# Folded Fourier weights and re-placed expert steps in a six-block macaron kernel

## The chip, the cores and the metric

The kernel runs on one core of one Trainium2 chip, all in float32. The metric is the time of the whole program on the device in microseconds (us), as the median of several runs; lower is better.

## The reference, cut to what matters

Six residual blocks run on x of shape (8, 256, 128): feed-forward 1 (six nodes of 8-head attention), attention, feed-forward 1 again, experts, a mixer, and the same experts again. The change touches the last three and the end of the block before them.

```python
# experts (twice): LN(x) -> top 2 of 8
logits = xf @ gate_w;  scores = softmax(logits);  top_scores, top_idx = top_k(scores, 2)
h = silu(xs @ w1) * (xs @ w3)          # xs = xf scaled by the gate of each expert
x = x + 0.5 * (h @ w2).sum(experts)

# mixer: LN(x)
xz = einsum('bld,ed->bel', hidden, in_proj_w)             # 2 * 256 channels
out, out_b = selective scans of xz, forwards and backwards (16 states a channel)
x, z = split(xz)
xf = fftn(x, axes=(-2, -1))                               # over channels and tokens
xc = concatenate([xf.real, xf.imag], axis=1)              # 512 channels
xc = silu(conv1d(xc, fft_conv_w, 5 taps) + fft_conv_b)
x_out = ifftn(complex(*split(xc)));  v = abs(x_out * max(silu(z)))
y = out + out_b reversed + whitened v
x = x + y @ out_proj_w
```

The transform over channels, the input projection and the 5-tap convolution are all linear. So the kernel never transforms channels at run time: it composes, once, the matrix that leads from the 128 model features through the projection and the channel transform into the 512 outputs of each convolution tap (`w["conv"]`).

## The kernel before, in words

The 2048 tokens are four chunks of 512 (`NCH` = 4, `CT` = 512), each of four tiles of 128 (`NT` = 4). Feed-forward, attention and feed-forward run one after the other, each with a loop over `i` in which the order on TensorE (PE), VectorE (DVE) and ScalarE (ACT) is written out by hand. A dictionary `beside` puts steps of the next block's start into chosen `i`: `for_experts` prepares chunk 0 of the experts (LN statistics, scaling, transposes) at 46, 47 and 48 of the second feed-forward block, whose loop ends at 50.

`experts_and_mixer` runs the last three blocks as one list of slots. `at(slot, f, ...)` files a step under a slot, before or (with `last=True`) after the slot's scan sums. In each slot i the order is: scan of unit i (DVE, L1187) with its product with C (POOL, L1189); the product of unit i+1 with B (`feed`, DVE, L1176); the steps filed before; in odd slots the sums over states (`sums`, PE, L1206); the steps filed after; then `spread(i+2, i+4)`, PE products that broadcast rows for later units (L1158), and the exponentials of unit i+4 on ACT (L1166). The order on PE, DVE, ACT and POOL is exactly this; the SP queue, which issues the DMAs, is ordered by the framework's planner. There are 128 units, 32 a chunk (slots 0 to 127). Negative slots are the head; slots from 128 are the tail.

In the head stand:

- `taps` (L820, L827), which builds the short convolutions' weights, slots -28 to -25;
- the first experts, `first.step(n)` in slot n - 25, n = -2 to 17. A step n does the hidden products of tile n (`hidden`: PE L967, gate product `hid` on DVE L972, silu on ACT L975, product on POOL), closes tile n-2 (`close`: PE L993, x on DVE L997) and transposes tile n-1 (`turn`: PE L984, ACT copy L985). `early` and `late` put the preparation of the next chunk between the steps: statistics, scaling, transposes (L921), logits (L926) with their exponential (L937), and gates (L942 to L956);
- the mixer's start for chunk 0: `normalize`, `features`, four `convolve` (L1050), two `gate` products (L1037), `silu`, `ranks` (L1080), `steps` (L1101), `softplus` (L1114), `delta` (L1121, with two `du` DMAs), `rows` (sixteen small DMAs for B and C of each direction);
- the Fourier weights: `fetch` loads a tap's 1 MB into the tag `f8` (two buffers), `transform` (L839) applies the channel transform to the projection, and `conv_weights(tap, i)` (L868) multiplies the two, ten times, in slots -10 to -1: four 128-row pieces each, read by ACT (L876, L879) or by two DVE instructions (L882, L883).

All these small products use one PSUM tile, tag `p`, with one buffer (`bank`), so that each waits until the one before has been read.

In the tail the second experts' steps stand in slots n + 129, and their preparation, chunk by chunk, is in the same `early` and `late`: chunk 0 in slots 125 to 128, chunks 1 to 3 between the steps. ACT holds one table of functions at a time: Silu, Exp and Ln, and Sqrt need different ones, and a load appears in the trace as ACT_TABLE_LOAD (1.28 us). `exponentials()` loads the one for Exp and Ln ahead of time, at the end of `silu` and of `magnitude`.

Of the kernel before, what the change touches and what calls it, by code (L numbers as in the profile page):

```python
# [758 lines left out]


# [4 lines left out]
def experts_and_mixer(nc, tc, ident, nhalf, x, cols, ins, w, expert_xT, store):  # L765
# [19 lines left out]
    with ExitStack() as ctx:  # L785
# [4 lines left out]
        A = pool.tile([P, 2, 2, 4, 4], F32, name="A")  # L790
        Af = A.rearrange("p r t i j -> p (r t i j)")
        nc.scalar.activation(Af, A_log, AF.Exp)
        nc.vector.tensor_scalar(Af, Af, -1.0, -1e-25, ALU.mult, ALU.min)
# [39 lines left out]
        def transform():  # L833


            pf = bank([P, 4, D])
            for k in range(4):
                for t in range(2):
                    nc.tensor.matmul(  # L839
                        pf[:, k, :],  # L840
                        fold["FA"][:, t, k * P : (k + 1) * P],
                        fold["in_x"][:, t, :],
                        start=(t == 0),
                        stop=(t == 1),
                    )
            fold["fw"] = fw = pool.tile([P, 2, 6, D], F32, tag="t3", name="fw")
            for h, scale in enumerate((1.0, 0.5)):
                nc.scalar.mul(fw[:, h, 0:4, :], pf, scale)
                nc.scalar.mul(fw[:, h, 4:6, :], pf[:, 2:4, :], -scale)

        def fetch(tap):
            if tap is None:
                fold["FA"] = pool.tile([P, 2, 2 * S], F32, tag="mag", name="s_FA")
                nc.sync.dma_start(out=fold["FA"], in_=ins["s_FA"])
                fold["in_x"] = pool.tile([P, 2, D], F32, tag="mix0", name="s_in_x")
                nc.sync.dma_start(out=fold["in_x"], in_=ins["s_in_x"])
                return
            fold[tap] = pool.tile([P, 4, 2 * DI], F32, tag="f8", name="s_fft", bufs=2)
            nc.sync.dma_start(out=fold[tap], in_=ins["s_fft"][:, tap])

        def conv_weights(tap, i):
# [5 lines left out]
            for k, part in enumerate(((0, 1, 2, 3), (4, 5, 0, 1))[i]):  # L867
                nc.tensor.matmul(  # L868
                    pw,
                    fold["fw"][:, int(tap != 2), part, :],  # L870
                    fold[tap][:, k, :],
                    start=(k == 0),
                    stop=(k == 3),
                )
# [12 lines left out]
        class Experts:  # L887

            def __init__(self, xT=None, store=None):
                self.store = store
                self.chunks = [{} for _ in range(NCH)]
                if xT is not None:
                    self.chunks[0]["xT"] = xT
                self.tiles = [{} for _ in range(NCH * NT)]

            def early(self, n):
                c, i = n // NT + 1, n % NT
                if not 0 <= c < NCH:  # L900
                    return
                got = self.chunks[c]
                if i == 0:
                    got["stats"] = ln_scales(nc, pool, nhalf, x[c], 1e-5)
                elif i == 1:
                    both = pool.tile([P, 2, CT], F32, tag="dA", name="xn_xT", bufs=4)
                    got["xn"] = both[:, 0, :].rearrange("p (t d) -> p t d", t=NT)
                    got["xT"] = both[:, 1, :]
                    ln_scaled(nc, x[c], got["xn"], got["stats"])
                elif i == 3:  # L910
                    self.gates(got)

            def late(self, n):
                c, i = n // NT + 1, n % NT
                if not 0 <= c < NCH:
                    return
                got = self.chunks[c]
                if i == 1:
                    pt = bank([P, NT, P])
                    for t in range(NT):  # L920
                        nc.tensor.transpose(pt[:, t, :], got["xn"][:, t, :], ident)  # L921
                    nc.scalar.copy(got["xT"], pt.rearrange("p t l -> p (t l)"))
                elif i == 2:
                    pg = bank([P, NT, E])
                    for t in range(NT):
                        nc.tensor.matmul(  # L926
                            pg[:, t, :],
                            got["xT"][:, t * P : (t + 1) * P],
                            w["gate"],
                            start=True,  # L930
                            stop=True,
                        )
                    nmax = pool.tile([P, NT, 1], F32, tag="nmax", name="nmax")
                    nc.vector.tensor_reduce(nmax, pg, AX.X, ALU.max)
                    got["eg"] = eg = pool.tile([P, NT, E], F32, tag="eg", name="eg")
                    nc.vector.tensor_tensor(eg, pg, nmax.to_broadcast([P, NT, E]), ALU.subtract)
                    nc.scalar.activation(eg, eg, AF.Exp)  # L937

            def gates(self, got):
                eg = got["eg"]  # L940
                den = pool.tile([P, NT, 1], F32, tag="den", name="den")
                nc.vector.tensor_reduce(den, eg, AX.X, ALU.add)  # L942
                nc.vector.reciprocal(den, den)

                sc = pool.tile([P, NT, 2 * E], F32, tag="sc", name="sc")
                nc.gpsimd.memset(sc[:, :, E:], -1.0)
                nc.vector.tensor_tensor(sc[:, :, 0:E], eg, den.to_broadcast([P, NT, E]), ALU.mult)
                best = pool.tile([P, NT, 8], F32, tag="best", name="best")
                for t in range(NT):
                    nc.vector.max(best[:, t, :], sc[:, t, 0:E])  # L950
                nc.vector.memset(best[:, :, 2:8], -1.0)
                mark = pool.tile([P, NT, 2 * E], F32, tag="mark", name="mark")
                for t in range(NT):
                    nc.vector.match_replace(mark[:, t, :], best[:, t, :], sc[:, t, :], -2.0)
                got["gate"] = gate = pool.tile([P, NT, E, 1], F32, tag="gate", name="gate", bufs=2)
                nc.vector.scalar_tensor_tensor(  # L956
                    gate[:, :, :, 0], mark[:, :, 0:E], -2.0, sc[:, :, 0:E], ALU.is_equal, ALU.mult
                )
# [43 lines left out]
            def step(self, n):  # L1002
                self.early(n)
                self.hidden(n)
                if 0 <= n - 1 < NCH * NT or 0 <= n - 2 < NCH * NT:
                    pa = ps.tile([P, 2, CT], F32, tag="a", bufs=1, name="pa")
                    self.close(n - 2, pa)
                    self.turn(n - 1, pa)
                self.late(n)
# [3 lines left out]
        def normalize(ch, part):  # L1013
# [6 lines left out]
            if h == 0:  # L1020
                got["xn"] = expert_xT.rearrange("p (t d) -> p t d", t=NT)
# [42 lines left out]
        def silu(*tiles):  # L1064
# [6 lines left out]
            exponentials()  # L1071
# [336 lines left out]
        first, second = Experts(xT=expert_xT), Experts(store=store)  # L1408
        for n in range(-NT, NCH * NT + 2):
            if n >= -2:  # L1410
                at(n - 25, first.step, n)
            at(n + NCH * UNITS + 1, second.step, n)
# [7 lines left out]
        for k, (tap, i) in enumerate(order):  # L1420
            at(-10 + k, conv_weights, tap, i)
            if i == 1 and k < 6:
                at(-10 + k, fetch, order[k + 4][0])

        for ch in range(NCH):

            o = (ch - 1) * UNITS
            if ch == 0:
# [6 lines left out]
                at(-10, gate, ch, 1)  # L1435
                at(-9, silu, u_of(ch, 0), u_of(ch, 1), sz_of(ch))
# [4 lines left out]
                at(-7, steps, ch, 0, 1, last=True)  # L1441
                at(-6, softplus, ch)
            else:
# [9 lines left out]
                at(o + 20, silu, u_of(ch, 0), u_of(ch, 1), sz_of(ch), sc_of(ch - 1, 0))  # L1453
                at(o + 21, largest, ch)
# [33 lines left out]
            at(k, silu, *(sc_of(ch, co) for co in range(0 if final else 1, 4)))  # L1488
            at(k + 1, halves, ch, 0)
# [54 lines left out]
    "s_FA": (P, 2, 2 * S),  # L1544
# [8 lines left out]
def tile_kernel(ctx: ExitStack, tc: tile.TileContext, ins, out):  # L1553
# [28 lines left out]
    expert_xT = cpool.tile([P, CT], F32, name="first0")  # L1582

    with tc.tile_pool(name="w_ffn", bufs=1) as fp:
        hand = [expert_xT, *(fp.tile([P, CT], F32, name=f"first{i}") for i in (1, 2))]
# [29 lines left out]
        def for_experts(ps, bufs):  # L1615
# [4 lines left out]
            to_features(nc, ps, ident, tiles[1], expert_xT, bufs=bufs)  # L1620
# [22 lines left out]
        ffn(nc, tc, ident, nhalf, x, made.w, hand[0], steps(for_experts, 46, 47, 48))  # L1643
    with tc.tile_pool(name="w_mixer", bufs=1) as wp:
# [4 lines left out]
        experts_and_mixer(nc, tc, ident, nhalf, x, cols, ins, w | w_moe, expert_xT, store)  # L1649


def layout(i):
# [52 lines left out]
    fft = tiles(np.transpose(i["L1_attn_fft_conv_w"], (1, 2, 0)))  # L1705
    a["s_fft"] = np.swapaxes(fft, 1, 2)
    phase = 2 * np.pi * (np.outer(np.arange(S), np.arange(S)) % S) / S
    c, s = np.cos(phase), np.sin(phase)
    a["s_FA"] = tiles(np.concatenate([c, -s], 1).astype(np.float32))
# [57 lines left out]
```

## Time and profile before

| What | Value |
|---|---|
| Median of 3 runs | 2143.36 us (2140.32 to 2144.17) |
| The profiled execution | 2135.52 us, its span 2133.7 us |
| Mean granted TensorE clock | 0.964 |
| PE, DVE, ACT, POOL busy | 92%, 73%, 54%, 37% of the span |
| Head: 1394 to 1490 us | PE busy 77.4 of 96 us, DVE 19.2, ACT 30.5, POOL 10.4 |
| Last units: 1984 to 2046 us | PE busy 53.8 of 62 us, DVE 48.9, ACT 26.4, POOL 50.8 |
| Tail: 2070 to 2134 us | PE busy 45.4 of 64 us, DVE 23.4, ACT 25.2, POOL 20.6 |

The page gives busy times over the whole span; the view by windows gives them for a stretch, with the granted clock; the chain of waits follows the work that ended last back to its releasers; the timeline lists instructions in order of time with the idle time ahead of each and who ended it. All times of views are counted from the start of the span.

### The profile page before, as it was taken

Reading aid. Unit: us, or ns where it says so; the run is one execution under the profiler, and the core shown is the slowest. Engines: PE = TensorE matmul, PEld = TensorE weight load, DVE = VectorE, ACT = ScalarE, POOL = GpSimd, SP = SyncE. Lnnn points to the kernel's source line nnn. Section 1 sums busy time; section 2 is a strip of 40 time slices with the busy share of each in tenths; the row PEclk is TensorE's granted clock in tenths of the full one; section 3 lists DMA queues with packets and bytes.
Section 4 is the critical chain, followed back from the end, with each engine's and each line's share of the span. In section 5 each row is a group of like instructions: output and inputs, shape, how many; then the busy total and the mean of one; then the engine's idle time right before and its main releaser. Section 6 shows DMA issues by size and latency. Waiting matters only on the chain.

```text
span 2133.7 us, 45254 instructions
## 1 busy us (share of the span) xinstructions
PE 1962.1 (92%) x17868; PEld 1140.0 (53%) x17868; DVE 1548.6 (73%) x2651; ACT 1155.7 (54%) x2206; POOL 797.5 (37%) x916
## 2 busy tenths in 40 slices
PE   7999999998999999999999997787898988989976
PEld 5666666654566666666666654542233334334444
DVE  5777777777877776777777785412987978888853
ACT  3777777752323322677777763433455555654543
POOL 3000001036666655000000013311758968778852
PEclk9999999999999999899999997999998999999989
DMA  3000000000000000000000002002001000010000
GB/s 140 3 3 3 3 3 3 3 3 1 2 2 2 2 2 2 2 3 3 3 3 3 3 2 88 0 25 64 10 11 30 1 20 21 2 39 1 1 6 16
DMA packets 21076, 28.32 MB, mean 13 GB/s; under 512 B 12352, under 2 KB 13888, under 8 KB 20224
## 3 DMA queue, kind: packets, MB, share of 16 engines
q1 hardware_dynamic: 20576, 25.22, 4.0%
q8 instruction: 142, 2.33, 0.5%
q14 instruction: 70, 0.57, 0.1%
q10 hardware_dynamic: 288, 0.20, 0.0%
HBM read 15.17 MB, written 1.05 MB: 8 GB/s over the span
## 4 chain that ended last, share of the span: by engine, by line
PE 79%; DVE 8%; ACT 6%; POOL 3%; issue 3%; DMA 1%; DVEq 0%; ACTq 0%; SPq 0%; POOLq 0%
PE sc L339 20%; PE pc L378 9%; PE sc L607 6%; PE pp L294 6%; PE pU L1158 4%; PE pc L666 3%; PE p L1250 3%; PE pp L578 2%; PE p L1050 2%; PE ph L967 2%; PE py L1206 2%; PE pp L312 2%; PE p L868 2%; DVE h L1187 2%; PE pp L419 2%
## 5 line engine op out<-in xcount | busy, mean ns | idle before, releaser
L345 DVE TENSOR_REDUCE negmax<-sc 128x2 f32<-128x512 f32 x768 | 490.8, 681 | 161.2 <-PE sc L339 160.9
L350 ACT ACTIVATE ex<-sc 128x512 f32<-128x512 f32 x768 | 421.0, 609 | 197.3 <-PE sc L339 196.9
L339 PE MATMUL sc<-qk,qk 32*128 32x256 f32 x6144 | 474.1, 407 | 8.6 <-DVE negmax L345 7.5
L339 PEld LDWEIGHTS sc<-qk,qk 32*128 32x128 f32 x6144 | 298.0, 187 | 144.4 <-ACT ex L350 102.8
L1189 POOL TENSOR_TENSOR hc<-h,C 128x1024 f32<-128x1024 f32 x128 | 301.5, 2359 | 103.5 <-DVE h L1187 97.8
L1187 DVE TENSOR_TENSOR_SCAN h<-dA,pU 128x1024 f32<-128x1024 f32 x128 | 292.1, 2282 | 15.3 <-POOL hc L1189 2.3
L300 ACT ACTIVATE qk<-pp,w_bqk,head_rows 128x256 f32<-128x256 f32 x384 | 197.2, 572 | 78.0 <-PE pp L420 34.6
L86 POOL TENSOR_SCALAR ln_ve<-ln_mv 128x2 f32<-128x2 f32 (+1 forms) x56 | 12.6, 224 | 582.3 <-DVE ln_mv L84 580.5
L1166 ACT ACTIVATE dA<-pA,A 128x512 f32<-128x512 f32 x256 | 161.9, 684 | 87.4 <-PE pA L1158 87.3
L378 PE MATMUL pc<-ex,va 128*32 128x256 f32 x3072 | 205.2, 385 | 0.2 <-DVE y L443 0.2
L1176 DVE TENSOR_TENSOR pU<-pU,B 128x1024 f32<-128x1024 f32 x128 | 155.5, 1215 | 59.2 <-PE pA L1158 58.7
L1158 PE MATMUL pU<-du,s_sel 32*128 32x512 f32 x512 | 166.8, 664 | 18.8 <-DVE h L1187 18.2
L622 ACT ACTIVATE ex<-sc 128x512 f32<-128x512 f32 x128 | 66.1, 603 | 205.1 <-PE sc L607 205.1
L1158 PE MATMUL pA<-dl,s_sel 32*128 32x512 f32 x512 | 152.9, 671 | 6.5 <-ACT dA L1166 6.5
L607 PE MATMUL sc<-rot,rot 32*128 32x256 f32 x2048 | 135.2, 388 | 1.9 <-POOL rot L590 1.9
L378 PEld LDWEIGHTS pc<-ex,va 128*32 128x32 f32 x3072 | 80.5, 109 | 96.0 <-issue 61.1
L607 PEld LDWEIGHTS sc<-rot,rot 32*128 32x128 f32 x2048 | 97.9, 184 | 36.8 <-issue 23.1
L199 POOL TENSOR_SCALAR w_bqk<-pb,head_rows 128x2 f32<-128x2 f32 x12 | 3.5, 314 | 302.1 <-DVE pb L196 295.2
L625 POOL TENSOR_TENSOR both<-ex 128x512 f32<-128x512 f32 x64 | 80.0, 1271 | 71.5 <-ACT ex L622 71.5
L1158 PEld LDWEIGHTS pU<-du,s_sel 32*128 32x128 f32 x512 | 48.2, 193 | 97.4 <-issue 77.2
L972 DVE TENSOR_TENSOR hid<-ph,gate 128x1024 f32<-128x1024 f32 x32 | 39.1, 1223 | 80.8 <-PE ph L967 79.4
L617 DVE TENSOR_REDUCE anegmax<-sc 128x2 f32<-128x512 f32 x128 | 79.4, 683 | 25.1 <-PE sc L607 25.1
(274 smaller groups left out, 3209.9 us busy)
## 6 DMA issues: line engine op xcount, KB each, us to landing
qk<-turned SPq DMA_DIRECT2D x768, 1.0 KB
s_fft<-s_fft SPq DMA_DIRECT2D x5, 1024.0 KB
du<-ab SPq DMA_DIRECT2D x16, 256.0 KB
B<-low SPq DMA_DIRECT2D x64, 32.0 KB
C<-low SPq DMA_DIRECT2D x64, 32.0 KB
x<-x SPq DMA_DIRECT2D x4, 256.0 KB
out<-x SPq DMA_DIRECT2D x4, 256.0 KB
weT<-ffn_weT SPq DMA_DIRECT2D x1, 960.0 KB
```

What stands on the lines that cost most here:

```text
L294: nc.tensor.matmul(pp, w["qk"][:, c, i, :], src, start=True, stop=True)
L300: nc.scalar.activation(t[:, g, :], pp, AF.Identity, scale=w["mask"][:, g : g + 1], bias=w["bqk"][:, c, i, g : g + 1],)
L339: nc.tensor.matmul(sc[:, t, :], lhs[:, t * P : (t + 1) * P], rhs, start=True, stop=True)
L345: nc.vector.tensor_reduce(sh[:, :, 4 * g + j], sc, AX.X, ALU.max, negate=True)
L350: nc.scalar.activation(ex, sc, AF.Exp, scale=FD**-0.5)
L378: nc.tensor.matmul(st["pc"][32 * j : 32 * j + 32, g, :], st[2][:, kt, 2 * j + g, :], st["ex", g, j][:, kt, :], start=(kt == 0), stop=(kt = ...
L607: nc.tensor.matmul(sc[j][:, t, :], lhs[r, part, t * P : (t + 1) * P] if part < 2 else sel[r, :], rhs[r, part, :] if part < 2 else st["nm"] ...
L1158: nc.tensor.matmul(dst[:, jj, :], w["sel"][rs, i, :], src[rs, :], start=True, stop=True)
L1166: nc.scalar.activation(dA[:, jj, :], pA[:, jj, :], AF.Exp, scale=A[:, r, t, i, j : j + 1])
L1176: nc.vector.tensor_tensor(dB, dB, bcast(gots[ch]["B", r], 2), ALU.mult)
L1187: nc.vector.tensor_tensor_scan(hf, af, bf, 0.0, ALU.mult, ALU.add)
L1189: nc.gpsimd.tensor_tensor(hc, h, bcast(gots[ch]["C", r], 2), ALU.mult)
```

## The change

It has three parts.

The Fourier weights. The input to the channel transform is real, so frequency 256 - f carries the conjugate of frequency f. The host now stores each tap's 512 input rows as frequencies 0 to 127 and the mirrored ones beside them, for the real and the imaginary half, and row 128 apart (`s_fft128`). `fold_pairs` adds two pieces (POOL), subtracts two others (DVE) and copies the row of frequency 128 into the row that is free (a DMA on SP). `conv_weights` then multiplies two pieces in place of four. The transform has three blocks in place of four. The folds stand in slots -8 to 1 and the products in -6 to 3, filed after the scan sums (before: -10 to -1, filed before).

The first experts' steps. Steps 0 to 11 stay in slots -25 to -14; steps 12 to 17 move from -13 to -8 into -10, -9, -8, -8, -7, -7. The silu of chunk 0 moves from -9 to -10, the second gate product from -10 to -11, and the Exp table is loaded in slot -6, ahead of softplus, and not right after that silu. Elsewhere `exponentials` is filed in the slot where `silu` called it.

The gates. `expert_logits` and `expert_gates` are functions now; their memset of -1.0 is on DVE and not on POOL. For chunk 0 of the first experts they run in the feed-forward block's `beside` (49 and 50). For chunks 1 to 3 statistics, scaling and transposes come one slot later, and logits and gates one after the other in the slot of i = 3. For the second experts chunks 0 to 2 are prepared in slots 119 to 123, 122 to 126 and 125 to 129 in buffers of other tags; chunk 3 stays between the steps. Besides, A is computed in place in `cols`.

```diff
+def expert_logits(nc, pool, pg, xT, w_gate):
+    for t in range(NT):
+        nc.tensor.matmul(pg[:, t, :], xT[:, t * P : (t + 1) * P], w_gate, start=True, stop=True)
+    nmax = pool.tile([P, NT, 1], F32, tag="nmax", name="nmax")
+    nc.vector.tensor_reduce(nmax, pg, AX.X, ALU.max)
...
+    nc.vector.tensor_tensor(eg, pg, nmax.to_broadcast([P, NT, E]), ALU.subtract)
+    nc.scalar.activation(eg, eg, AF.Exp)
...
         def transform():
-            pf = bank([P, 4, D])
-            for k in range(4):
+            pf = bank([P, 3, D])
+            for k in range(3):
...
             for h, scale in enumerate((1.0, 0.5)):
-                nc.scalar.mul(fw[:, h, 0:4, :], pf, scale)
-                nc.scalar.mul(fw[:, h, 4:6, :], pf[:, 2:4, :], -scale)
+                nc.scalar.mul(fold["fw"][:, h], pf, scale)
...
+        def fold_pairs(n, tap, i):
+            got = fold[tap]
+            to = fold["room"][:, 1 + n % 3].rearrange("p (k o) -> p k o", k=2)
+            fold["pairs", tap, i] = to
+            j = 2 * i
+            nc.gpsimd.tensor_tensor(to[:, 0], got[:, j], got[:, j + 1], ALU.add)
+            j = 2 - j
+            nc.vector.tensor_tensor(to[:, 1], got[:, j], got[:, j + 1], ALU.subtract)
+            nc.sync.dma_start(out=to[0:1, 1], in_=ins["s_fft128"][:, tap, i])
+
         def conv_weights(tap, i):
             pw = bank([P, 2 * DI])
-            for k, part in enumerate(((0, 1, 2, 3), (4, 5, 0, 1))[i]):
+            for k in range(2):
                 nc.tensor.matmul(
                     pw,
-                    fold["fw"][:, int(tap != 2), part, :],
-                    fold[tap][:, k, :],
+                    fold["fw"][:, int(tap != 2), (1 + i) * k, :],
+                    fold["pairs", tap, i][:, k],
                     start=(k == 0),
-                    stop=(k == 3),
+                    stop=(k == 1),
                 )
...
             def step(self, n):
-                self.early(n)
                 self.hidden(n)
...
-                self.late(n)
...
-        first, second = Experts(xT=expert_xT), Experts(store=store)
-        for n in range(-NT, NCH * NT + 2):
-            if n >= -2:
-                at(n - 25, first.step, n)
-            at(n + NCH * UNITS + 1, second.step, n)
+        first, second = Experts(given=given), Experts(store=store)
+        lead = dict(zip(range(18), (-25, -24, -23, -22, -21, -20, -19, -18, -17, -16, -15, -14)))
+        lead |= dict(zip(range(12, 18), (-10, -9, -8, -8, -7, -7)))
+        for n in range(-3, NCH * NT + 2):
+            c, i = n // NT + 1, n % NT
+            k = lead.get(n, n - 25)
+            if 0 < c < NCH and i == 1:
+                at(k, first.statistics, c)
+            if 0 < c < NCH and i == 2:
+                at(k, first.scale, c)
+            if n >= 0:
+                at(k, first.step, n)
+            if 0 < c < NCH and i == 2:
+                at(k, first.transpose, c)
+            if 0 < c < NCH and i == 3:
+                at(k, first.logits, c)
+                at(k, first.gates, c)
...
+        end = NCH * UNITS
+        for c in range(3):
+            k = end - 9 + 3 * c
+            at(k, second.statistics, c)
+            at(k + 1, second.scale, c, room)
+            at(k + 2, second.transpose, c)
+            at(k + 3, second.logits, c)
+            at(k + 4, second.gates, c)
+        for n in range(NCH * NT + 2):
+            k = n + end + 1
...
+            at(k, second.step, n)
...
         for k, (tap, i) in enumerate(order):
-            at(-10 + k, conv_weights, tap, i)
+            at(-8 + k, fold_pairs, k, tap, i)
+            at(-6 + k, conv_weights, tap, i, last=True)
             if i == 1 and k < 6:
-                at(-10 + k, fetch, order[k + 4][0])
+                at(-8 + k, fetch, order[k + 4][0])
...
-                at(-10, gate, ch, 1)
-                at(-9, silu, u_of(ch, 0), u_of(ch, 1), sz_of(ch))
+                at(-11, gate, ch, 1)
+                at(-10, silu, u_of(ch, 0), u_of(ch, 1), sz_of(ch))
...
+                at(-6, exponentials)
                 at(-6, softplus, ch)
...
-        ffn(nc, tc, ident, nhalf, x, made.w, hand[0], steps(for_experts, 46, 47, 48))
+        ffn(nc, tc, ident, nhalf, x, made.w, hand[0], steps(for_experts, 46, 47, 48, 49, 50))
```

## The prediction

> **What bounds the kernel now.** I read the page first, for the engines.
>
> ```profile
> PE 1962.1 (92%) x17868; PEld 1140.0 (53%) x17868; DVE 1548.6 (73%) x2651; ACT 1155.7 (54%) x2206; POOL 797.5 (37%) x916
> ```
>
> TensorE (PE) is busy 92% of the span, but this is an average over stages, and the change touches only the last: the end of the second feed-forward block (about 1300 to 1311 us), the head of the mixer (1311 until unit 1's scan at 1492.8), the first scan units, and the tail with the second experts (2000 to 2130). So next I read the chain of waits by windows. In the head:
>
> ```profile
> 1417.72 3.45 PE p L868 x8
> 1421.19 0.59 ACT w_conv L876
> 1421.83 1.13 PE p L1037 x2
> ...
> 1449.50 0.59 ACT dl L1110
> 1450.13 6.72 PE p L868 x8
> 1456.94 0.69 DVE w_conv L882
> 1457.63 0.61 DVE w_conv L883
> 1458.29 3.71 PE p L868 x8
> ...
> 1492.78 2.29 DVE h L1187
> 1495.07 1.13 DVE pU L1176
> ```
>
> L868 is the Fourier weights' product. There are ten, and all stand on the chain. Every product, its read and the next user of the one PSUM tile `p` follow one another (3.45 + 0.59 us, or 3.71 + 1.30). From 1492.78 the chain is DVE alone: scan 2.29 and pU 1.13, one unit each 3.54 us. So before slot 0 time on PE counts; after it, time on DVE does.
>
> One product took 6.72. The view by windows tells why (last columns: granted clock, DMA share, GB/s):
>
> ```profile
> 1445.80:1449.20 3.40, 1.62 (x4) 0.29 (x2) 0.00 (x0) 1.65 (x3) 0.00 (x0) 1.00 0.81 313
> 1449.20:1456.90 7.70, 6.71 (x8) 2.52 (x8) 0.00 (x0) 2.88 (x4) 0.00 (x0) 0.56 0.15 35
> ```
>
> After 3.4 us in which PE worked 1.62 us, the granted clock fell to half for the next 7 us. In the tail the chain reads:
>
> ```profile
> 2063.32 0.68 DVE mark L954 x5
> 2064.22 1.13 DVE hid L972
> 2065.70 1.09 PE pa L984 x4
> 2066.78 3.43 PE ph L967 x4
> ...
> 2092.01 1.22 DVE hid L972
> 2093.58 0.63 PE pa L984 x4
> 2094.21 1.73 PE ph L967 x4
> 2096.03 1.23 DVE hid L972
> ```
>
> A plain experts' step takes 4.0 us (hid at 2092.01 and 2096.03). Where a chunk's gates (`mark`) come ahead of `hid`, it takes more.
>
> **The change, part by part.** Durations are from this execution.
>
> *End of the block, first units.* Chunk 0's logits and gates leave slots -27 and -26. The logits held PE and `p` from 1314.99 to 1317.47: -2.5. They go into the block's drain, where PE is idle. The gates (DVE, 2.0 us by the rows 2104.88 to 2107.06) come after the last statistics (end 1308.2) and ahead of `yn`, which begins at 1309.3: +0.8, since the mixer's first DMA waits for what follows `yn`. The transform has 12 matmul instructions in place of 16 (2.05 us): -0.5. The memset to -1.0 moves from POOL to DVE, 0.1 us a chunk. Together -2.2; bounds -4 and +1.
>
> *Head, up to slot 0.* I take T = 1390.52, the start of the last convolve that keeps its place after step 11. Before, unit 1's spread starts at 1490.25 = T + 99.7. After, in the new order, each PE piece with its read where the next one needs `p`:
> - three convolves (3.44 + 0.96 until ACT has read) and two gate products (1.8, 1.1) with no steps between them: T + 16.1;
> - steps 12 and 13 (4.1 each) and ranks 0 (1.7): 26.0; the silus (2.9 on ACT) lie beside step 13;
> - steps 14 and 15 (8.2), ranks 1 (1.8), and the remainders 16 and 17 (3.6): 39.6;
> - two step-size products of 2.5 (1447.65 to 1450.13): 44.5;
> - the first folded weight: two of four matmuls, so 1.72 + 0.2; its read stands on ACT behind the table load (1.28) and softplus (2.1): 48.3;
> - weight 2.6, steps 2.6, weight 2.6, steps 2.5, weight 2.6: 61.2;
> - weight with DVE read 3.4, frequencies 1.7, weight 3.3, frequencies 1.3: T + 70.9.
>
> That is -28.8. Cross-check: the ten products cost 49.2 us of chain before (4.11, 4.05, 4.37, 4.38, 8.16, 5.08, 4.37, 4.38, 5.15, 5.15). Six remain ahead of slot 0, at about 17.5, so -31.7; some 3 us come back because steps no longer hide the convolves' reads.
>
> The folds cost the path nothing here. The add (POOL) is nearest to L976, 1.27; the subtract (DVE) to half of L1121's 1.21, 0.6. Both are two slots early, and DVE is idle 77 of 96 us. The 2 KB row DMA follows the subtract on SP's queue: issue 0.5 to 0.6 (rows L1126, L1127), landing under the 2.6 of s_inT, against about 10 us of lead. If that cover is gone, +6: SP has four row copies of 5.3 us each in the same stretch, and an issue that waits holds all behind it, the `du` copies too (8 us of slack).
>
> Clock: from T + 36 to T + 44.6 PE works about 4.5 of 8.6 us, as little as before 1449.20, so I expect half clock for the first two weights: +2.5. The first one's loss hides behind softplus. Bounds: 0, and +14 if all six weights and the step products run slow. The Trainium skill, "TensorE: Matmul & The Clock Gate", Part 1, puts the drop after about 3.4 us of idle; the rows above show it with no idle stretch over 1.4 us. By the page's figure this term would be 0 and the forecast 2.5 us lower.
>
> Head: -26.3; bounds -31 and -12.
>
> *Units 0 to 3.* Four weights and two folds land here. Slots 0 and 1: a DVE subtract each, +0.6 and +0.7. Slot 2: PE has a convolve 3.7, a wait for its read 0.8, the weight 1.9; DVE stands idle behind scan and feed (3.5) until 6.4, then reads 1.3. Slot 3: DVE reads 1.3 more. Units 2 to 4 thus start 12.5 us apart in place of 7.1: +5.4. Together +6.7; bounds 3.7 (DVE work alone) and 12.
>
> *Tail.* Chunks 1 and 2 are prepared in slots 122 to 129 and not between steps. Chunk 1: `hid` 2, 3, 4 stand at 2054.0, 2064.1, 2070.2. Without its transposes, two table loads of 1.28 and gates, ACT gets to `hid` 2 at 2058.0, and `hid` 4 follows 9.5 after `hid` 2, not 16.2: -6.7, the half-clock `ph` of 3.43 included. Chunk 2: `hid` 6 to 7 takes 6.5, not 4.0, and its transposes hold the output product 1.4: -3.9. Chunk 3 stays. Paid for: slots 119 to 127 run at DVE's pace (3.54), and statistics (1.6), nmax and eg (0.4) and gates (2.0) of two more chunks are added there: 7.8, and 1 for PE's transposes and logits. But before, 9.9 us lay between the last scan's end (2036.16) and the first `ph`: PE waited for chunk 0's scales, then ran at half clock. Chunk 2 now sits there one slot later, and I estimate 5: -5. Sum -10.6 + 8.8 - 5 = -6.8; bounds -12 and +3.
>
> *Sum.* -2.2 - 26.3 + 6.7 - 6.8 = -28.6. The profiled execution took 2135.5 (span 2133.7 and 1.8 around it), 7.9 under the median of 2143.4. So 2106.9 in its terms, 2115 as a median.
>
> **Rivals.**
> 1. *The tail gives nothing.* Prepared early, the gates cost the DVE-bound units what they save later, and the gap after the scans stays at 9.9. For it: 3.54 us a unit without idle time. Against: chunk 1's 16.2. 2115 + 6.8 = 2122.
> 2. *A new queue in front of the first units.* SP's rows come late (+6) and units 0 to 3 cost 12 (+5.3): 2126. For it: SP stood 25 us behind one wait for `dl` before its `du` copies. Against: none of that reached PE.
> 3. *The clock, slower than before.* With half the matmuls gone and the reads still there, PE falls below the busy share that keeps the clock, from step 12 to unit 3. About 51 us of matmuls lie in those 76 us; at half clock they add 51, less what the 24 us of waits hide, so 27 to 51. I take 33, since most waits are in the serial chain but many products overlap other engines: 2115 + 33 = 2148. It decides only from half clock over some seven eighths of the stretch; at half of it the gain is still 12. For it: 7.7 us at 0.56 here, and 0.51 from 1514 to 1524. Against: weights at 1.9 in 2.6 are busier than the 1.62 in 3.40 that tripped it. The skill's same page, "A second HAM failure mode: psum-queue depth-cycling", describes this: short idles between groups make the clock swing.
> 4. *More than forecast.* Full clock throughout, and the tail at its bound: 2115 - 2.5 - 5 - 4.5 (steps hiding reads) = 2103.
> 5. *The fold halves nothing:* the fetched tile keeps its 1 MB. But the matmul count falls from 40 to 20, so hardly.
>
> **How the numbers follow.** Forecast 0.45, rival 1 0.15, rival 2 0.20, rival 3 0.07, rival 4 0.11, rival 5 0.02. The range 2101 to 2134 reaches from rival 4 past rival 2 and leaves out rival 3, rival 5 and parts of the ends. A measurement here tells 0.2%, 4.3 us, from no change. Faster by more: all but rivals 3 and 5, 0.91, less the near ends of rival 2: 0.89. Within: 0.04. Slower: rival 3 and unforeseen waits, 0.07.
>
> **What would show it.** Right: L868 with 40 records; unit 1's spread about 26 us earlier counted from the convolve at T (28 counted from the start of the span); units 2 to 4 12.5 us apart; no gates between `hid` 0 and `hid` 8; `hid` 3 to 4 near 4. Wrong: L868 records of 1.2 us in most weights, PE waiting for the s_fft128 DMA, DVE waiting between scans of slots 119 to 127 for logits, or a span within 10 us of 2133.7.

## The result, and the profile after

The changed kernel takes 2126.4 us (median of 4 runs, 2123.64 to 2129.53) against 2143.25: a ratio of 0.9924, 95% interval 0.9907 to 0.9941. It is faster by 16.9 us, where 28 were forecast. Its profiled execution took 2127.31 us, span 2125.5, so by the two traces the gain is 8.2 us only: the traced execution of before lay 7.7 under this median of four, this one 0.9 above its own.

So I cut both traces at the same events: the first hidden product `ph` of the experts, the first step-size product (L1101, now L1114), and the scans of units 0, 4, 85 and 127. The last two rows end at the second experts' first `hid` and at the end of the span.

| Stretch (us) | before | after | difference | forecast |
|---|---|---|---|---|
| start to first `ph` | 1322.2 | 1318.5 | -3.6 | about -2 |
| first `ph` to step-size product | 123.0 | 107.8 | -15.2 | |
| to scan 0 | 43.3 | 40.9 | -2.4 | |
| scan 0 to 4 | 15.0 | 23.4 | +8.4 | +6.7 |
| (first `ph` to scan 4) | 181.2 | 172.1 | -9.2 | -20.1 |
| scan 4 to 85 | 347.3 | 349.9 | +2.7 | 0 |
| scan 85 to 127 | 183.2 | 200.4 | +17.2 | +8.8 |
| scan 127 to first `hid` | 13.9 | 7.9 | -6.0 | -5 |
| first `hid` to end | 85.9 | 76.6 | -9.3 | -10.6 |

Eleven microseconds are missing ahead of scan 4, and the tail (the last three rows: +1.9 in place of -6.8) gives nothing. Now the views, in the order in which they answer those of before. The page, engines:

```profile
PE 1952.2 (92%) x17824; PEld 1129.7 (53%) x17824; DVE 1558.5 (73%) x2669; ACT 1151.2 (54%) x2200; POOL 810.5 (38%) x918
```

PE does 10 us less; the share is still 92%. The view of line L916, the folded product (L868 before, which had 80 records and a median of 592 ns):

```profile
L916 PE MATMUL p<-fw_pairs x40: 592/668/1193, 1431.4 to 1488.7; 128*128 128x512 f32 x40
```

The count halved, 40 records, but the median rose and the slowest took twice the shortest. The view by windows shows where (columns: PE, PEld, DVE, ACT, POOL busy, granted clock, DMA share, GB/s):

```profile
1424.00:1431.30 7.30, 3.90 (x16) 1.89 (x16) 1.49 (x3) 3.16 (x6) 1.58 (x2) 0.93 0.43 130
1431.30:1440.00 8.70, 7.50 (x8) 2.35 (x8) 2.13 (x3) 4.25 (x5) 3.90 (x6) 0.50 0.13 44
1440.00:1450.00 10.00, 7.08 (x10) 2.17 (x10) 1.96 (x5) 2.14 (x4) 3.15 (x3) 0.50 0.56 174
1450.00:1456.00 6.00, 4.55 (x6) 1.34 (x5) 0.25 (x2) 2.53 (x4) 1.37 (x4) 0.50 0.54 186
1456.00:1470.00 14.00, 11.66 (x40) 4.27 (x39) 9.39 (x14) 6.06 (x10) 4.27 (x7) 0.94 0.05 11
```

After 7.3 us in which PE worked 3.9, the clock is halved for 25 us. So the first folded products take as long as the whole ones did (timeline of PE, then of ACT):

```profile
1431.39 3.75 PE L916 MATMUL p<-fw_pairs 128*128 128x512 f32 x4 [1.45 <-ACT dl L1123]
1435.91 3.75 PE L916 MATMUL p<-fw_pairs 128*128 128x512 f32 x4 [0.77 <-ACT w_conv L924]
...
1444.99 3.75 PE L916 MATMUL p<-fw_pairs 128*128 128x512 f32 x4 [2.58 <-ACT dl L1123]
1448.67 2.08 PE L1171 MATMUL pA<-dl,s_sel 32*128 32x512 f32 x4
1450.68 2.07 PE L1114 MATMUL p<-low,s_dtT 64*128 64x512 f32 x2
```

```profile
1443.58 0.69 ACT L1122 ACTIVATE ab<-p,cols 128x512 f32<-128x512 f32 x1 [3.30 <-DMA du<-ab]
```

This ACT line has a wait that the prediction did not have. `ab` is one buffer: the step sizes of the second half overwrite what the two `du` DMAs of the first half are still reading. ACT stands 3.30 us, the step-size product's read with it, and PE 2.58 behind that.

In units 0 to 3 (DVE), the wait came where it was expected, behind the convolve of slot 2, and was longer:

```profile
1476.39 2.27 DVE L1200 TENSOR_TENSOR_SCAN h<-dA,pU 128x1024 f32<-128x1024 f32 x1
...
1484.38 0.69 DVE L930 TENSOR_TENSOR w_conv<-p,first 128x512 f32<-128x512 f32 x1 [4.59 <-PE p L916]
...
1490.62 2.28 DVE L1200 TENSOR_TENSOR_SCAN h<-dA,pU 128x1024 f32<-128x1024 f32 x1
```

Units 2 to 4 lie 14.2 us apart (12.5 forecast, 7.1 before). Around the last scans PE waits for others (timelines of POOL, PE and DVE):

```profile
2002.06 2.35 POOL L1289 TENSOR_TENSOR sp<-fsc 128x1024 f32<-128x1024 f32 x1
```

```profile
2004.46 1.22 PE L1295 MATMUL p<-s_G,sp 128*128 128x256 f32 x2 [2.67 <-POOL sp L1289]
...
2031.67 1.19 PE L1295 MATMUL p<-s_G,t 128*128 128x256 f32 x2 [1.86 <-DVE eg L769]
```

```profile
2020.89 1.99 DVE L782 TENSOR_TENSOR sc<-eg,den 128x32 f32<-128x32 f32 x1
```

Chunk 0's LN chain stands on POOL just ahead of `halves` (sp). The logits hold the one tile `p` until DVE reads it behind a scan and a feed. And a gate product that takes 0.19 us elsewhere took 1.99: it ended at 2022.88, when POOL's product with C (2020.48, 2.35 us) ended at 2022.83. Behind the scans no gates come between `hid` 0 and `hid` 8. Most of these steps are 4.0 us apart, but the step from `hid` 3 to `hid` 4 took 7.23 (a plain one follows it): PE waited 1.72 us for an ACT copy, and its `ph` took 3.02 us at half clock:

```profile
2058.73 1.21 DVE L987 TENSOR_TENSOR hid<-ph,gate 128x1024 f32<-128x1024 f32 x1
2065.96 1.23 DVE L987 TENSOR_TENSOR hid<-ph,gate 128x1024 f32<-128x1024 f32 x1 [4.16 <-PE ph L982]
2069.99 1.23 DVE L987 TENSOR_TENSOR hid<-ph,gate 128x1024 f32<-128x1024 f32 x1 [2.60 <-PE ph L982]
```

### The profile page after: what moved, and what is told of

It is laid out like the page before. It is cut to its first block, busy times and chain, and to the rows that moved or that the text cites. A ratio compares the mean times of both kernels' runs of the same rounds, so it can differ in the third digit from the quotient of the medians.

```text
span 2125.5 us, 45202 instructions
## 1 busy us (share of the span) xinstructions
PE 1952.2 (92%) x17824; PEld 1129.7 (53%) x17824; DVE 1558.5 (73%) x2669; ACT 1151.2 (54%) x2200; POOL 810.5 (38%) x918
## 5 line engine op out<-in xcount | busy, mean ns | idle before, releaser
L86 POOL TENSOR_SCALAR ln_ve<-ln_mv 128x2 f32<-128x2 f32 (+1 forms) x56 | 12.5, 224 | 567.0 <-DVE ln_mv L84 562.1
L1179 ACT ACTIVATE dA<-pA,cols 128x512 f32<-128x512 f32 x256 | 162.1, 684 | 96.4 <-PE pA L1171 95.8
```

Of the source, the lines that this page charges most:

```text
L1179: nc.scalar.activation(dA[:, jj, :], pA[:, jj, :], AF.Exp, scale=A[:, r, t, i, j : j + 1])
```

## The experiments

The kernel before took 2135.8 to 2142.6 us on the chips of these runs, so I compare ratios to it, each with an interval of about 0.002 to 0.003 to either side (4 to 6 us), and the stretches of the traces. Code that the kernels share takes the same time in most stretches to 0.1 us. Some stretches vary with the same code: the start up to the first `ph` (1313.5 to 1321.5 us), from there to the step-size product (105.6 to 107.9), from that to scan 0 (39.3 to 40.9), scans 4 to 85 (340 to 350), and the old steps behind the first `hid` (86.0 to 87.5).

**The fold alone.** Onto the kernel before; weights, steps, gates and tail keep their places.

```diff
+            at(-12 + k, fold_pairs, k, tap, i)
             at(-10 + k, conv_weights, tap, i)
```

> The kernel before with the fold alone: two products of half the frequencies in place of four, each Fourier weight in its old slot (-10 to -1), experts' steps, gates and tail as before. By the prediction's terms each of the ten products falls from 3.45 to 1.72 us on TensorE's serial chain, and the transform by 0.5: 10 x 1.72 + 0.5 = 17.7 us less, so about 2125.6 us, as fast as the whole change; the new places of weights, steps and gates would then be worth nothing. Rival, the clock: with less work between the same reads the granted clock falls to about 0.5 in the weights' stretch, as it did in the whole change (3.75 us for a folded product), and the fold alone gives between 0 and 8 us, 2135 to 2143.

2126.85 us, ratio 0.9933 (0.9907 to 0.9960). From first `ph` to scan 4 it takes 167.1 us: 14.2 less than before, and 5.0 less than the whole change.

```profile
1435.74 1.95 PE L882 MATMUL p<-fw_pairs 128*128 128x512 f32 x4 [0.76 <-ACT low L1097]
1443.41 3.35 PE L882 MATMUL p<-fw_pairs 128*128 128x512 f32 x4 [1.45 <-ACT dl L1124]
...
1463.33 3.63 PE L882 MATMUL p<-fw_pairs 128*128 128x512 f32 x4 [0.39 <-ACT dl L1124]
```

Eight of its ten products take 1.88 to 1.96 us, two fall into half clock, 3.1 us in all, which is most of what is missing from 17.7. So the fold alone has as much of the gain as the whole change by time. What the change did besides cost 5 us up to scan 4, by the traces.

**The old tail.** The changed kernel with chunks 0 to 3 of the second experts prepared as before.

```diff
+            if 0 <= c < NCH and i == 0:
+                at(k, second.statistics, c)
...
             at(k, second.step, n)
+            if 0 <= c < NCH and i == 1:
+                at(k, second.transpose, c)
```

> The changed kernel with the second experts' chunks prepared as before (chunk 0 in slots 125 to 128, chunks 1 to 3 between the steps); all else as changed. By the prediction's term the new places are worth 6.8 us, so this kernel would take about 2133 us. By the two traces they gave 15.3 us after the last scan and cost 16.25 between scan 119 and scan 127: worth nothing, 2126 us plus or minus 2.5, with scan 127 about 16 us earlier and the end 15 us longer.

2127.24 us, ratio 0.9934 (0.9909 to 0.9960). Scan 85 to the end takes 285.6 us, with the new tail 284.9 (in the trace of before it was 283.1): the tail part is worth nothing that can be told, as the traces had it.

**Fillers that keep TensorE busy.** The first of the two suspects in the head.

```diff
+        def warm(count):
+            pw = ps.tile([P, 2, CT], F32, tag="u", name="warm")
+            for k in range(count):
+                nc.tensor.matmul(pw[:, k, :], w["inT"][:, 0:P], xTm, start=True, stop=True)
+        at(-7, warm, 1)
+        for k in (-7, -6, -5):
+            at(k, warm, 1, last=True)
+        at(-4, warm, 2)
+        at(-3, warm, 1)
```

> The changed kernel with seven additional matmuls of 512 columns, whose results nobody reads, in TensorE's idle gaps of slots -7 to -3. Clock theory: the granted clock stays at 1 from 1424 us on, a folded product takes 1.9 instead of 3.75 us, and unit 0's scan starts 4 to 6 us earlier (2121 to 2123 us); not more, since ScalarE's wait for the transfer that reads the tile ab (until 1443.6 us) is untouched. Rival: the stretch is bound by the chain of softplus, ab and the du transfers, and the fillers give nothing or cost up to 5 us (2126 to 2131).

2122.37 us, ratio 0.9918 (0.9897 to 0.9940), not to be told from the change's 0.9924. From the step-size product to scan 0 it takes 41.0 us, not less than 40.9: my clock theory, as I put it, fell. That the median lies in its range of 2121 to 2123 is luck: the trace is 4.9 us shorter than that of the change, and 5.0 of them are the start up to the first `ph`, where the code is the same. The lines (PE, ACT) say why the stretch gained nothing:

```profile
1430.38 1.95 PE L916 MATMUL p<-fw_pairs 128*128 128x512 f32 x4 [1.12 <-ACT w_conv L924]
...
1440.04 3.75 PE L916 MATMUL p<-fw_pairs 128*128 128x512 f32 x4 [3.88 <-ACT dl L1123]
```

```profile
1438.63 0.69 ACT L1122 ACTIVATE ab<-p,cols 128x512 f32<-128x512 f32 x1 [5.67 <-DMA du<-ab]
```

The first two products take 1.95, but what they saved turned into a longer wait for `ab` (5.67 for 3.30), in which PE idles 3.88 and the clock falls after all.

**A second `ab`.** The other suspect: the buffer of the second half lies in another tag.

```diff
-                got["ab"] = pool.tile([P, 2, CT], F32, tag="ab", name="ab")
+                tag = "mag" if ch == 0 and t == 1 else "ab"
+                got["ab"] = pool.tile([P, 2, CT], F32, tag=tag, name="ab")
```

> The changed kernel with the second ab tile alone. Theory: TensorE's 2.58 us of idle time ahead of the third Fourier weight, which followed ScalarE's 3.30 us wait for the du transfers, go, and unit 0's scan starts 2 to 3 us earlier; the granted clock stays at half from 1431 to 1456 us: about 2124. Rival: the six Fourier weights at half clock are the longer chain and take up the wait, so the time stays within 1 us of 2126.4.

2123.74 us, ratio 0.9943 (0.9922 to 0.9963): by time no gain can be told. By stretches, 36.2 us from step-size product to scan 0, 4.7 less and more than I expected; four weights still take 2.9 to 3.75 us.

**Both.** The second `ab` and six fillers (one, not two, in slot -4).

> The changed kernel with both edits of the head: the second ab tile (as in i_after_ab) and six additional matmuls that nobody reads in slots -7 to -3. From the first step-size product to unit 0's scan the changed kernel took 40.9 us; with the fillers alone 41.0, since ScalarE's wait for ab grew by what the weights saved; with the second tile alone 36.2, with TensorE still at half clock in four of the six weights. Theory: the two causes hide each other, and only both edits bring what the prediction worked out for this stretch without them: the clock stays at full, the weights take 1.9 to 2.0 us, and the stretch takes 29 to 32 us, so 9 to 12 us less than the changed kernel, about 2116. Rival: the stretch is bound by another chain (the du transfers, or VectorE's reads of the weights) and stays at 35 to 37 us; or the clock falls in spite of the fillers.

2114.97 us, ratio 0.9892 (0.9873 to 0.9912). 31.3 us from step-size product to scan 0, and 161.0 from first `ph` to scan 4, 20.2 less than before, where the prediction had 20.1 (with 2.5 for the clock taken off).

```profile
1440.00:1456.00 16.00, 13.19 (x39) 4.25 (x37) 8.96 (x18) 8.40 (x13) 6.48 (x11) 1.00 0.49 163
```

```profile
L916 PE MATMUL p<-fw_pairs x40: 592/593/697, 1429.7 to 1477.4; 128*128 128x512 f32 x40
```

The clock is at full throughout, and a folded matmul takes 593 ns. Each of the two causes hid the other, in whole or in part: in this stretch the edits gave 0 and 4.7 us alone, together 9.6.

**The weights earlier.** All ten inside the first experts' steps 6 to 15, where PE waits for DVE; folds two steps ahead.

```diff
                     self.close(n - 2, pa)
+                    if between is not None:
+                        conv_weights(*between)
                     self.turn(n - 1, pa)
...
-            at(-8 + k, fold_pairs, k, tap, i)
-            at(-6 + k, conv_weights, tap, i, last=True)
+            at(lead[4 + k], fold_pairs, k, tap, i)
```

> The changed kernel with all ten Fourier weights made earlier, each inside one experts' step (steps 6 to 15), between the step's closing product and its transposes, where TensorE waited 0.8 us for VectorE; folds two steps ahead. Theory: a product of 1.9 us costs 1.1 there, 11 us in all, at full clock; nothing of them is left from slot -6 to slot 3, where the six and four of them now cost about 27 us and 9 us. What remains there is the chain from the step sizes to the first scan (about 24 us from the first step-size product), so unit 0 starts about 6 us earlier, units 0 to 3 are 9 us shorter: about 15 us less than the changed kernel, 2111 us (2107 to 2117). Rival: a product costs 2.6 us there as between other users of the tile p, so that 26 us are added, and the time stays within 3 us of 2126.

2108.47 us, ratio 0.9861 (0.9831 to 0.9890). By stretches: first `ph` to step-size product +10.4 against the change (11 expected), to scan 0 -13.0, scans 0 to 4 -8.2, so -10.8 up to scan 4. The products run at full clock, and the one shown has no wait ahead of it (view of line, then the timeline):

```profile
L916 PE MATMUL p<-fw_pairs x40: 592/592/595, 1350.9 to 1428.0; 128*128 128x512 f32 x40
```

```profile
1385.40 1.05 PE L1008 MATMUL pa<-m_w,sg_hT 128*128 128x128 f32 x8
1386.30 1.88 PE L916 MATMUL p<-fw_pairs 128*128 128x512 f32 x4
1388.01 0.60 PE L999 MATMUL pa<-ident,sg_hT 128*128 128x128 f32 x4
```

Another 8.0 came in scans 4 to 85 (341.9 for 349.9), which no theory had. There the clock's falls lie elsewhere: slot 30 took 9.32 us at a granted 0.72 in the changed kernel, 6.49 at 1.00 here. The early weights alone do not settle it: a later run has them and took 348.1. And ACT's wait for `ab` is now the longest of the head:

```profile
1452.49 0.69 ACT L1124 ACTIVATE ab<-p,cols 128x512 f32<-128x512 f32 x1 [8.37 <-DMA du<-ab]
```

**Early weights and a second `ab`.**

> The kernel d_weights_early with a second tile for ab in the first chunk's second half, so that ScalarE's Abs of steps (1, 0) doesn't wait 8.37 us for the du transfers that read the first. Theory: this wait held the step-size product, both spreads behind it on TensorE and so unit 0; the next latest is the landing of du itself (1452.5 us), unit 0's scan starts 3 to 7 us earlier: about 2103.5. Rival: unit 0 waits for du anyway, and nothing changes (2108.5 plus or minus 2).

2107.46 us on a chip where before took 2137.6: ratio 0.9861 (0.9834 to 0.9888), no gain that the time tells. The stretch to scan 0 falls from 27.9 to 24.1, the 3 to 7 us expected.

**Chunks 0 and 1 of the tail in DVE's waits.** On the early weights; slots 85 to 99, and ACT copies the logits out of PSUM.

```diff
+        slots = ((85, 87, 91, 93, 93), (93, 95, 96, 97, 99), (125, 126, 127, 128, 129))
```

> The kernel d_weights_early with the second experts' chunks 0 and 1 prepared in slots 85 to 99 instead of 119 to 126, where VectorE waits for the spread (5.6 us ahead of the feed in slot 86, 4.0 in slot 94, 2.7 in slot 100); chunk 2 stays in slots 125 to 129. The logits of the three chunks are first copied from PSUM by ScalarE. Theory: of the 16.3 us that the three preparations cost between scans 119 and 127, those of chunks 0 and 1 go (about 11 to 12), and come back as at most 3 in slots 85 to 99: 8 to 12 us less than d_weights_early (2108.5), about 2098. Rival: VectorE's own 8 us for the two chunks have to be paid wherever they lie, so the time stays within 3 us of 2108.5 and scans 85 to 99 spread out by as much.

2109.93 us, ratio 0.9871 (0.9849 to 0.9894): the rival had the time right. Scans 85 to 127 take 193.6 in place of 200.5, so 10.4 of the 17.2 us are still paid, all of them in units 85 to 119 (160.8 us; before, 150.4). One reason is argued and not shown by itself: DVE's idle time there is a wait for a spread, the spread waits for the scan before, and a later scan only moves the wait. Another came with the copy: DVE waits 2.72 us for the second copied logits, and the small subtractions that read the copies take 1.29 and 2.12 us, where they took 0.19 reading `p`. A gate product takes 1.82. What the slots would have cost without the copy, no run shows. And the gap from scan 127 to the first `hid` is back at 13.8 (7.9): 6.9 won, 5.9 lost.

**Both edits.**

> The two edits of f_tail_slack and g_second_ab together on d_weights_early. Theory: the gains lie in different stretches and add: 2108.5 - 10 - 5 = 2093 (2089 to 2098). Rival: one of the two gives nothing by its own rival, then 2098 to 2104.

2106.56 us, ratio 0.9863 (0.9841 to 0.9885), where about 2093 was expected. The two do add in their own stretches (24.1 and 284.1), but the tail's was only 1.0 to begin with. Its trace shows what fills the gap (PE):

```profile
2013.75 1.63 PE L966 MATMUL p<-ident,exn 128*128 128x128 f32 x4 [2.93 <-ACT exn L117]
2015.31 1.94 PE L1225 MATMUL py<-hc,s_ysel 128*32 128x512 f32 x8
```

PE waits 2.93 us for chunk 2's scaled tokens, and then runs at about half clock while the transform's last products (over_tokens) queue behind.

**Logits copied early.** The changed kernel; `expert_logits` copies to SBUF on ACT for chunks 0 to 2 of the second experts.

```diff
+    if copy:
+        nc.scalar.copy(eg, pg)
+        pg = eg
```

> The changed kernel, with ScalarE copying the logits of the second experts' chunks 0 to 2 from the PSUM tile p to SBUF at once, so that TensorE's next user of p doesn't wait for VectorE to read them behind a scan and a feed. Theory 1, a slot lost between scans 119 and 127 is lost at the end: the waits for p (1.86 us and the half clock behind it) go, scan 127 and the end come 3 to 5 us earlier, 2122. Theory 2, the stretch from scan 119 to the experts' first hid is set by the other branch's chain (folds, over_tokens, magnitude) with chunk 2's statistics in it, and slow scans only hide that: scan 127 comes 3 to 5 us earlier, the gap from scan 127 to the first hid (7.9 us) grows by as much, and the time stays within 1 us of 2126.4.

2126.96 us, ratio 0.9951 (0.9934 to 0.9968). Scans 110 to 127 take 85.5 for 87.6, the gap to the first `hid` 10.5 for 7.9, and scan 85 to the end 284.5 for 284.9: theory 2 in kind, smaller than expected in size. The copy has a price that neither theory had. Here is the same subtraction, in the changed kernel from `p` and in this run from the copy, both beside POOL's product with C (2030.94, 2.35 us, and 2028.30, 2.34 us):

```profile
2031.33 0.19 DVE L769 TENSOR_TENSOR eg<-p,nmax 128x32 f32<-128x32 f32 x1
```

```profile
2028.68 2.01 DVE L772 TENSOR_TENSOR eg<-eg,nmax 128x32 f32<-128x32 f32 x1
```

**Chunk 2 out of the gap.** On the kernel with both edits.

```diff
-        slots = ((85, 87, 91, 93, 93), (93, 95, 96, 97, 99), (125, 126, 127, 128, 129))
+        slots = ((85, 87, 91, 93, 93), (93, 95, 96, 97, 99), (120, 122, 129, 130, 131))
...
+            at(k3, second.logits, c, last=c == 2)
```

> The kernel h_all with chunk 2 of the second experts spread out: statistics in slot 120, scale in 122, transposes and logits behind the first two experts' steps (slots 129 and 130, where the Exp table is loaded anyway), gates in 131. Theory 2: in h_all the gap of 13.8 us from scan 127 to the first hid holds TensorE's 2.9 us wait for chunk 2's scaled tokens, behind which it ran at half clock, and chunk 2's logits and gates; without them the gap falls to 8 to 10 us, slot 120 pays 1.6 for the statistics, the steps behind 1 to 2: 2 to 4 us less than h_all from scan 110 to the end. Rival: the gap is that of the over_tokens products alone, and nothing changes.

2100.73 us, ratio 0.9848 (0.9822 to 0.9874): 0.8% below the change (0.9848 / 0.9924), and not to be told by time from the kernel it was built on (0.9863). Scan 85 to the end takes 279.3 us, 4.8 less than in the kernel it was built on and the only one of all that is under 280; the gap is 6.0:

```profile
2015.49 1.23 DVE L990 TENSOR_TENSOR hid<-ph,gate 128x1024 f32<-128x1024 f32 x1 [3.70 <-PE ph L985]
```

**And fillers.**

> The kernel k_chunk2_late with eight additional matmuls of 512 columns, read by nobody, from the step-size products to the first spread. Clock theory: the spreads and products from 1445 to 1459 us run at 1.0 to 1.1 instead of 2.1 us, and unit 0's scan starts 2 to 3 us earlier, counted from the first step-size product; the time is 2 to 3 us below k_chunk2_late. Rival: unit 0 waits for the landing of du, which is not TensorE's, and gains under 1 us.

2103.99 us, ratio 0.9846 (0.9823 to 0.9868). By time nothing is gained. The stretch to scan 0 falls from 24.1 to 21.8, as expected; but scans 0 to 4 take 1.2 more, and scans 4 to 85 348.1 for 340.3, in code that is the same. Slot 30 in this kernel, then in the one without fillers:

```profile
1582.43:1591.80 9.37, 9.37 (x36) 5.16 (x36) 4.15 (x7) 3.56 (x6) 5.07 (x6) 0.71 0.00 0
```

```profile
1576.86:1583.34 6.48, 6.12 (x35) 3.89 (x28) 4.15 (x8) 3.10 (x6) 5.06 (x6) 1.00 0.00 0
```

So some 8 us of the middle units hang on where the clock falls. What decides that is not shown: the five traces with early weights and no fillers took 340 to 342 us, the nine others 347 to 350.

## Why the prediction was right and wrong

*The direction and the fold* were right: 20 in place of 40 products, 3.45 to 1.9 us each at full clock, and the fold alone has the whole gain of the change by time (0.9933 to 0.9924). Rival 5 is out. But one of the prediction's signs of being wrong came too: the span, 2125.5 us, lies within 10 us of 2133.7. Unit 1's spread came 83.5 us behind the convolve at T, some 16 us earlier than before and not 26.

*The end of the block and the first units*: chunk 0's gates came ahead of `yn` and cost 0.8 as worked out; the first `ph` came 3.6 us earlier (2.2), but with the same code it varies by 8.

*The head* is the step that failed. With clock and `ab` mended, the stretch up to scan 4 is 20.2 us shorter, where 20.1 were forecast; but the forecast had 2.5 for the clock in it, so its other terms came to 22.6 and were 2.4 too good, 1.7 of them in units 0 to 3. Two terms were mis-sized by more. The clock, put at +2.5 with a bound of +14: I let it cover the first two weights and hid one of them behind softplus; it stayed at half from 1431 to 1456. And `ab`, put at nothing: I let steps (1, 0) run 2.6 us behind weight 2, and did not ask whether its output buffer was free. I gave the `du` copies 8 us of slack towards those who read `du`; the next writer of `ab` left them none. Moving the experts' steps away left little but that chain, in which both showed; with the steps in place, the fold alone had only two of ten products at half clock. Together they took 9.6 us behind the step-size product. The mended kernel is shorter by another 1.5 ahead of it, but that lies before either edit: a convolve that took 5.37 us in the changed kernel, partly at half clock, and 3.67 there.

The Trainium skill, "TensorE: Matmul & The Clock Gate", Part 1, says that the clock halves after an idle window of about 3.4 us and comes back after a busy one. By the first half no fall was due here: no idle stretch of PE between 1402 and 1431 us exceeds 1.45 us. By the second it should have come back by 1453, since PE's rows follow one another without a gap from 1444.99 to 1452.75, longer than two such windows; it came back after 1456. For the fall, the runs speak for the busy share: after 53% busy (3.90 of 7.30) it fell, at 82% (13.19 of 16.00, fillers and second `ab`) it held.

*Units 0 to 3*: +8.4 against +6.7, inside the bounds; the clock has no part in it, since with it mended the stretch is 23.4 too. The convolve, the wait for its read and the weight follow one another as worked out; but the convolve began 1.35 us behind scan 2 (1477.74 against 1476.39), behind a spread, which the prediction put at nothing.

*The tail*: what the steps save was nearly right (-9.3 for -10.6). `hid` 4 follows 11.3 us behind `hid` 2, not 9.5, in part since the half-clock `ph` that was to go stayed (3.02 us); so the sign "`hid` 3 to 4 near 4" did not come (7.23). The gap was right in size (-6.0 for -5), but not for the reason given. The gap did not fall because chunk 2 sat there one slot later; it fell because the scans ahead were slower, so that the transform's products (halves, over_channels, over_tokens) were further on when they ended. Where the scans were faster (chunks 0 and 1 early, logits copied) the gap grew by about as much. Chunk 2's own work in the gap counts too: with it spread out, the gap was 6.0 behind fast scans, and the steps behind it took 3.0 more.

The price in the last units was mis-sized: 17.2 for 8.8 (two chunks of 4.0 us are 8.0 and not 7.8, which changes little). I had summed DVE's work; to it came POOL's LN chain ahead of `halves`, `p` held by logits, and PE at half clock behind both. Of these only the hold on `p` was taken away by itself, for about 2 us of scans 110 to 127, and the copy that did it brought its own stall; the shares of the others are not shown. Rival 1 thus got the tail right, by another mechanism.

The stalled gate product is one more part of it: the Trainium skill, "SBUF — State Buffer", "Who interferes with whom", says that a DVE instruction with two SBUF inputs and a POOL one that reads SBUF hold one port in turn, whole instruction by whole instruction; the 1.99 us for 0.19, ending within 0.05 us of POOL's product, agree. So does the subtraction above: 0.19 us from PSUM beside POOL's product, 2.01 with both inputs in SBUF, ending at 2030.69 when that product ended at 2030.64. What the stall costs the end of the kernel no run shows.

*Rival 2* has the number that was measured, 2126, but not the mechanism: no PE wait in the trace ends with a row of s_fft128. *Rival 3* named one of the two causes of the head, at several times its price.

*Open*: the medians differ by 16.9 us, the traces by 8.2. The 8.7 between them lie in executions that were not traced. That scans 4 to 85 take 340 to 350 us by where the clock falls could account for part of it, but is not shown for the kernel before.

## What to carry to other kernels

Before work is moved out of a chain of waits, ask of each step left in it whether its output buffer is free, not only whether its inputs are there; and ask what share of the time TensorE will then be busy. When two causes follow each other in a chain, taking one away can show little: take both away in one run before either is called harmless. Idle time of the engine that bounds a stretch is no room when the engine waits, through another, for itself; and a gap behind a loop should be costed with the branch that runs beside the loop.

## What the runs showed of the hardware

The granted clock fell to half with PE busy about half the time (3.90 of 7.30 us) and no idle stretch above 1.45 us, and stayed there for 25 us at a busy share of 71 to 86% counted in half-clock durations; six unread products of 1.1 us each, with the second `ab`, kept it at full. The two `du` DMAs (128 partitions between them, SBUF to SBUF) held their source for about 4 us from the second issue (1448.38 until ACT could write at 1452.49, with the weights early; 1439.34 to 1443.58 in the changed kernel), so a buffer read by a DMA is busy far longer than the engine that wrote it suggests. A DVE subtraction of 128x32 took 0.19 us with an input in PSUM and 2.01 with both in SBUF, each beside a POOL product of 2.34 to 2.35 us.
